# A planned Winograd kernel on Trainium2: the planner gives each PSUM bank one reader at a time, and four smaller edits

## The chip, the cores and the metric

The kernel runs on one core of a Trainium2 chip. The metric is the device time of one execution in microseconds. The engines are named as in the profile: PE is TensorE's matmul and PEld its weight load, DVE is VectorE, ACT is ScalarE, POOL is GpSimd, and SP is SyncE, which issues most transfers.

## The reference

`x` is 1024 x 512, `weight` is 64 x 512 x 512 (embedding e, feature f, model m), `lin_w` is 512 x 512, all in fp32:

```python
out_lin = x @ lin_w.T + lin_b
xv = jnp.einsum('bf,efm->bem', x, weight)
zp = jnp.einsum('bf,efm->bem', jnp.square(x), jnp.square(weight))
interaction = 0.5 * jnp.sum(jnp.square(xv) - zp, axis=1)
return out_lin + interaction
```

The second product needs no e of its own: the sum over e of x^2 times w^2 is x^2 times the sum of w^2 over e. So the large work is `xv`, whose squares are summed over e.

## The kernel before, in words

**Tiles and groups.** The 512 columns m are cut into 22 groups (`groups`, line 149): two narrow ones of 16 columns and twenty wide ones of 24. With the 64 embeddings, half a wide group is 12 x 64 = 768 columns of weights. The batch is cut into two halves of 512 rows (four blocks of 128), the features into two halves of 256 (two blocks of 128).

**Outer level.** Of each group, the 2 x 2 blocks of x times the 2 x 2 blocks of the weight are multiplied with seven products in place of eight (Winograd's form of Strassen's scheme), numbered 1 to 7 and run in the `ORDER` 1, 6, 5, 2, 7, 4, 3 (line 19). The sums of blocks of x (`X1` to `X7`) are made once. The sums of weights come by DMAs that add into SBUF (`outer_sum`, line 696, through `dma_add`, line 470), issued from GpSimd's queue; so do two sums of results (`outer_out`, line 707: ob += od after product 7's tree, oc += od after product 4's).

**Inner level.** Each outer product has a tree of its own. Products 6, 4 and 3 of every group, and all seven of a narrow one, go through `tree` (line 737): seven inner products of two matmuls each, 384 columns in a wide group. Products 1, 5, 2 and 7 of wide groups go through `wide_tree` (line 826): twenty inner products of one matmul of 256 columns. The sums of weight pieces (tile `t`) are made on GpSimd. fp32 matmuls stand in the profile as two records each.

**PSUM.** Four tiles `b1`, `b3`, `b2_0`, `b2_1` of two banks each take the products. The single banks are `b_l` and `b_r` in the profile (`alone=True`, line 379), the pair is `b`. A product is added in place onto what a bank holds; what must be kept is copied to another bank or to SBUF (`p5`, `p53`: `p` in the profile) by ScalarE (`copy`, line 443, shown as L446 or L447), and results leave by VectorE's adds (`tt`, line 429, shown as L437), which may also run on GpSimd when no operand is in PSUM. Matmuls are at line 480, or 537 for the two ends.

**`EARLY` and `HOLD`.** For outer products in `EARLY` (line 21), `tree` adds the addend of the result's last quarter to bank b3 right after inner product 5 (`leave(3, "b3")`, line 797) and adds bank b2 later (`more(3, b2)`, line 817). For the others, line 799 copies b3 to a p5 tile and line 819 adds bank and tile first, then the addend. Product 4's addend is `oc`, its target `oa` (lines 732 and 733).

**After the trees.** ScalarE squares the results and VectorE sums the squares over e into `acc` (`finish`, line 722, shown as L454 and L463). `w_squares` (line 713) does the same to the raw weights, into `w2_sum`.

**The two ends.** `lin` (line 614) computes the linear part first, and the end (from line 1005) computes x^2 times `w2_sum`, both by `outer_products` (line 595): seven products `big` (line 529) of sixteen records each per block product, on pairs of banks, with the copies u2 <- b1 and u3 <- u2 between them. At the end the linear part and half of `acc` are first added up (`add_acc`, line 1048, shown as L1051), the sums of squares of x are made by `tt` and `minus_both` (line 581, shown as L584, VectorE alone), and `leave` (line 1088) adds the products and stores the output.

**What sets the order.** No order is written by hand. `Plan` (line 153) holds every operation with a cost per engine, and `order` (line 191) plays the engines against each other and emits the operations in the order that comes out; on the chip each engine then runs its own in that order. PE's operations have keys (their place in the sequence) and may run ahead of it by at most `AHEAD` = 20 us when a lower key is not ready. For all others the planner works out the latest start that does not hold up PE, moved by the table `AHEAD_OF` (line 41, in eighths of a us by operation). `ready` (line 231) tells when an operation can start:

```python
        def ready(o):
            return max([0.0] + [d.end for d in o.waits]) + self.HOP
```

It knows of data and of buffers, not of two engines that read one bank at the same time. In the emitted program two such readers do run one after the other, as the trace shows. `APART` (line 252 and 258) keeps VectorE's operations of two SBUF operands that are marked `both` apart from GpSimd's; `add_acc` isn't marked.

Of the kernel before, what the change touches and what calls it, by code (L numbers as in the profile page):

```python
# [20 lines left out]
EARLY = (2, 4, 6, 7)  # L21
# [20 lines left out]
0:c 1:348h 2:2hcy 3:347k 4:3498 5:2hq1 6:2hlv 7:2h68 8:1muu 9:2h1k a:1mst b:2haa c:1wij d:2gyq e:1qxb f:l05  # L42
g:yb9 h:1aj i:5b4 j:29s4 k:-16 l:b m:l n:6 o:-v p:g q:2t r:d s:-9 t:-l u:1t v:ts w:1a x:c y:-n z:19 10:-k
11:4uw 12:-a 13:-10 14:-37 15:1o 16:n 17:-x 18:-14 19:m 1a:13 1b:-g 1c:18 1d:-6 1e:90j 1f:-e 1g:-1f 1h:3n 1i:i
1j:39 1k:-2z 1l:e 1m:-i 1n:-1g 1o:m 1p:35 1q:n 1r:-1 1s:-u 1t:-g 1u:13 1v:-3 1w:-2 1x:-3u 1y:-18 1z:-9 20:-2
21:s 22:m 23:-h 24:-y 25:u 26:-d 27:-31 28:3 29:u 2a:h 2b:17 2c:-s 2d:-o 2e:s 2f:b 2g:14 2h:1q 2i:26 2j:-i
2k:1i 2l:-4 2m:-2f 2n:z 2o:9 2p:-4 2q:15 2r:46 2s:44 2t:q 2u:-a 2v:-q 2w:-a 2x:1r 2y:-1m 2z:g 30:-19 31:-2o
32:8 33:14 34:-b 35:17 36:1t 37:-14 38:6 39:3 3a:-o 3b:-2 3c:-1o 3d:17 3e:-19 3f:1a3 3g:-7 3h:i 3i:-1j 3j:1md
3k:-15 3l:x 3m:128 3n:r 3o:-a 3p:-13 3q:-8 3r:h 3s:b 3t:-16 3u:-a 3v:1mh 3w:-9 3x:4 3y:-14 3z:-e 40:1t8 41:-f
42:e 43:1p 44:-k 45:1l 46:1g 47:-4 48:m 49:-13 4a:12 4b:-d 4c:-24 4d:-k 4e:r 4f:1 4g:-z 4h:i 4i:h 4j:1i 4k:c  # L50
4l:g 4m:9 4n:o 4o:-1f 4p:1e 4q:-3 4r:-1i 4s:f 4t:x 4u:-f 4v:-18 4w:-12 4x:1p8 4y:q 4z:-2e 50:-w 51:9 52:-1j
53:-10 54:5 55:3 56:1fd 57:r 58:a 59:1 5a:-12 5b:-2 5c:-6 5d:1r 5e:l 5f:-27 5g:8 5h:-15 5i:-5 5j:-n 5k:2g 5l:a
5m:-o 5n:p 5o:10 5p:1 5q:1b 5r:-l 5s:1bb 5t:-1 5u:-1o 5v:10 5w:-1 5x:2y 5y:-3 5z:5 60:1d 61:15 62:-d 63:5
64:-5 65:x 66:d 67:3 68:-w 69:-1r 6a:-z 6b:v 6c:ct 6d:-2t 6e:-j 6f:-2 6g:-6 6h:-t 6i:r 6j:-1f 6k:f 6l:d 6m:-1n
6n:b 6o:9 6p:5 6q:-5 6r:-22 6s:-3 6t:j 6u:-f 6v:h 6w:-6 6x:p 6y:-d 6z:-l 70:m 71:-c 72:-x 73:-y 74:-d 75:-v
76:m 77:-1 78:7 79:1a 7a:22 7b:a 7c:-2 7d:-v 7e:-2 7f:-k 7g:g 7h:-z 7i:-18 7j:-1b 7k:-13 7l:-17 7m:-o 7n:-u
7o:h 7p:z 7q:-5 7r:j 7s:-v 7t:6 7u:-u 7v:s 7w:i 7x:-v 7y:-1e 7z:-f 80:s 81:u 83:-j 84:-m 85:-7 86:-1e 87:f
88:2 89:1 8a:-1c 8b:-g 8c:-4 8d:-1y 8e:-j 8f:-u 8g:-5 8h:c 8i:-6 8j:-2 8k:-3 8l:-3 8m:-l 8n:s 8o:1c 8p:h
8q:-2e 8r:-e 8s:96 8t:-3 8u:6 8v:18 8w:17 8x:-3 8y:-1g 8z:-3 90:-5 91:-r 92:18 93:-1 94:3c 95:12 96:-s 97:-3
98:-15 99:p 9a:-e 9b:-15 9c:1b 9d:-1f 9e:9 9f:13 9g:g 9h:1k 9i:-17 9j:12 9k:b 9l:-28 9m:d 9n:c 9o:-6 9p:-5  # L60
9q:1 9r:-f 9s:x 9t:3 9u:-q 9v:12 9w:-13 9x:-q 9y:-r 9z:-u a0:-18 a1:-a a2:-8 a3:-1h a4:-17 a5:-w a6:1pg a7:-d
a8:-1 a9:-1c aa:-j ab:1a ac:e ad:-x ae:-6 af:-i ag:i ah:z ai:r aj:1r ak:8 al:-1h am:-35 an:-c ao:-5 ap:-z aq:x
ar:3 as:e at:1 au:g av:-c aw:w ax:-j ay:-u az:1r b0:6 b1:38 b2:1v b3:j b4:-10 b5:4 b6:15 b7:33 b8:-1 b9:-1
ba:-1d bb:1f bc:-2q bd:-c be:-16 bf:-c bg:1dx bh:18 bi:a bj:b bk:t bl:2 bm:8 bn:1x bo:-r bp:-o bq:f br:11
bs:-i bt:-2 bu:9 bv:-1x bw:-h bx:b by:-y bz:s c0:7 c1:1b c2:1v c3:i c4:-m c5:q c6:11 c7:7 c8:-x c9:-y ca:3
cb:d cc:-1p cd:1 ce:a cf:-1l cg:-17 ch:-q ci:-3 cj:56 ck:f cl:-1z cm:s cn:-1f co:w cp:-u cq:i cr:j cs:12 ct:5
cu:y cv:-l cw:-k cx:1 cy:-1e cz:-q d0:k d1:r d2:d d3:x d4:-q d5:-10 d6:o d7:-5 d8:1q d9:-r da:-a db:-2 dc:d
dd:-3 de:-3 df:-1p dg:-16 dh:l di:-l dj:-3q dk:18 dm:g dn:1y do:-z dp:-4 dq:-4 dr:-1c ds:c dt:-17 du:-fq dv:-a
dw:-bz dx:1m dy:-j dz:-1e e0:-20 e1:1s e2:1l e3:-1w e4:-1p e5:4 e6:j e7:-x e8:-19 e9:19 ea:1n eb:1g ec:-3
ee:13 ef:15 eg:-1o eh:-19 ei:2m ej:i ek:-x el:1d em:-a en:-4 eo:1i ep:-1z eq:-1t er:-1a es:15 eu:-c ev:a  # L70
ew:-1s ex:1f ey:2m ez:-t f0:1c f1:-y f2:-8 f3:g f4:-4 f5:-1m f6:83 f7:3 f8:-173 f9:t fa:-d fb:a fc:4 fd:20n
fe:b ff:-v fg:t fh:-n fi:34 fj:fq fk:-o fl:-l fm:-3 fn:-10 fo:-g fp:197 fq:e fr:-1g fs:1y ft:z fu:-w fv:-2v
fw:l fx:-1b fy:-1x fz:-19 g0:-l g1:-2 g2:36 g3:g g4:g g5:s g6:-5 g7:x g8:24 g9:m ga:h gb:q gc:-8 gd:o ge:-14
gf:f gg:-z gh:1 gi:k gj:-8 gk:v gl:19j gm:-d gn:z go:9 gp:a gq:i gr:-2 gs:-6 gt:6 gu:-1s gv:e gw:15 gx:-2
# [64 lines left out]
1ce:-c 1cf:x 1cg:12 1ch:4 1ci:-w 1cj:15 1ck:-2d 1cl:-f 1cm:-13 1cn:-21 1co:12 1cp:-32 1cq:-1j 1cr:2g 1cs:-1x  # L139
1ct:-6 1cu:-a 1cv:k 1cw:-l 1cx:n 1cy:i 1cz:-1t 1d1:14 1d2:-i 1d3:-q 1d4:-p 1d5:-k 1d6:-p 1d7:-4 1d8:-1 1d9:15  # L140
1da:-1z 1db:18 1dc:-9 1dd:s 1de:k 1df:-u 1dg:z 1dh:-f 1di:bj 1dj:-5 1dk:26 1dl:1 1dm:-6 1dn:8 1do:n 1dp:-d
1dq:-3 1dr:-28 1ds:x 1dt:n 1du:-c 1dv:j 1dw:v
"""
AHEAD = 20.0
APART = True
# [1009 lines left out]
```

## Time and profile before

| what | us |
|---|---|
| median of 3 runs | 1438.69 |
| lowest and highest run | 1434.45, 1439.11 |
| the profiled execution | 1437.59 |
| its span in the profile | 1435.8 |
| PE busy | 1409.5 |
| DVE busy | 1224.1 |
| POOL busy | 1088.4 |
| ACT busy | 792.7 |

The span is the time from the first to the last instruction of the profiled execution, whose own time is a little longer. The granted TensorE clock was 0.999 of full speed. In the rows that follow, a timeline row reads: start and length in us, engine, line, operation, what it writes and reads, shape, how often, and in brackets the engine's idle time before it with what ended it. A row of groups ends with busy us, mean ns of one, and the idle time before them. A row of waits gives the total, the number and the longest. A row of the chain gives start, length and what ran. A row of stretches gives the stretch, its length, then the busy time of PE, PEld, DVE, ACT and POOL with the number of records, the granted clock, the DMA share and GB/s.

### The profile page before, as it was taken

The numbers are of one execution on the slowest core, as the hardware profiler recorded it, in microseconds if no ns is written. First come the engines' busy times: TensorE is split into PE (matmuls) and PEld (weight loads), VectorE is DVE, ScalarE is ACT, GpSimd is POOL, SyncE is SP. The second block draws the span as 40 slices with busy tenths as digits, with TensorE's granted clock in tenths as the row PEclk, the third lists the DMA queues.
The fourth block names the chain that finished last, engine by engine and source line by source line (L and its number), as shares of the span: only waits on it lengthen the run. The fifth ranks groups of instructions, "written<-read, shape, count | busy, mean of one in ns | idle before, by whom it ended". The sixth has DMA issues, their size and how long they took to land.

```text
span 1435.8 us, 17687 instructions
## 1 busy us (share of the span) xinstructions
PE 1409.5 (98%) x5504; PEld 1024.8 (71%) x5504; DVE 1224.1 (85%) x1809; ACT 792.7 (55%) x1296; POOL 1088.4 (76%) x1067
## 2 busy tenths in 40 slices
PE   9999999999999999999999999999999999999988
PEld 7777767767676776767677676767677676767756
DVE  6577888888988888898889889888988988988887
ACT  3255465656646565665656465555646555565732
POOL 6999876877687777778787777778777687778760
PEclk9999999999999999999999999999999999999999
DMA  8779577684948678495957859595775959485672
GB/s 259 177 167 236 144 180 175 161 217 107 251 124 209 156 180 196 115 246 118 233 145 172 202 128 235 112 250 130 182 190 145 218 117 260 114 199 146 168 174 81
DMA packets 98542, 251.84 MB, mean 175 GB/s; under 512 B 29521, under 2 KB 39249, under 8 KB 98449
## 3 DMA queue, kind: packets, MB, share of 16 engines
q0 software_dynamic: 26448, 134.49, 48.0%
q1 hardware_dynamic: 70848, 115.17, 23.0%
q10 hardware_dynamic: 1152, 1.05, 0.2%
q8 instruction: 45, 0.74, 0.2%
q14 instruction: 49, 0.39, 0.1%
HBM read 127.04 MB, written 6.19 MB: 93 GB/s over the span
## 4 chain that ended last, share of the span: by engine, by line
PE 80%; POOL 6%; DMA 6%; DVE 3%; ACT 3%; issue 2%; SPq 0%; ACTq 0%; POOLq 0%; DVEq 0%
PE b L480 36%; PE b_r L480 22%; PE b_l L480 20%; POOL t L437 3%; PE b L537 2%; DVE oa L437 2%; POOL X L437 1%; DMA oc<-od 1%; DMA ob<-od 1%; DMA w<-T 1%; DMA ob<-lin_wT 1%; ACT b_l L447 1%; DVE w_sum L463 1%; DMA T<-weight 1%; ACT od L446 1%
## 5 line engine op out<-in xcount | busy, mean ns | idle before, releaser
L480 PE MATMUL b<-t,X 128*128 128x384 f32 (+1 forms) x1184 | 400.7, 471 | 5.9 <-DVE oa L437 3.4
L437 POOL TENSOR_TENSOR t<-t,w 128x512 f32<-128x512 f32 (+1 forms) x300 | 294.9, 991 | 113.2 <-PE b L480 86.8
L480 PEld LDWEIGHTS b<-t,X 128*128 128x128 f32 x1184 | 218.8, 190 | 133.6 <-POOL t L437 12.7
L480 PE MATMUL b_l<-t,X 128*128 128x256 f32 x960 | 247.6, 381 | 0.4 <-ACT b_l L447 0.3
L480 PE MATMUL b_r<-t,X 128*128 128x256 f32 x800 | 225.6, 386 | 3.7 <-ACT b_l L447 1.1
L480 PEld LDWEIGHTS b_l<-t,X 128*128 128x128 f32 x960 | 180.7, 190 | 37.9 <-ACT b_l L447 5.5
L437 POOL TENSOR_TENSOR t<-w 128x768 f32<-128x768 f32 (+1 forms) x88 | 162.9, 1851 | 50.5 <-DMA w<-T 28.9
L480 PEld LDWEIGHTS b_r<-t,X 128*128 128x128 f32 x800 | 145.6, 190 | 60.3 <-issue 16.2
L454 ACT ACTIVATE oa<-oa 128x768 f32<-128x768 f32 (+1 forms) x176 | 143.8, 824 | 78.5 <-DVE oa L437 77.8
L454 ACT ACTIVATE wsq<-w 128x768 f32<-128x768 f32 (+1 forms) x132 | 108.5, 823 | 127.0 <-DMA w<-weight 85.3
L463 DVE TENSOR_REDUCE w_sum<-wsq 128x12 f32<-128x768 f32 (+1 forms) x176 | 161.4, 920 | 1.5 <-ACT wsq L454 1.0
L463 DVE TENSOR_REDUCE acc<-oa 128x12 f32<-128x768 f32 (+1 forms) x176 | 158.5, 920 | 4.0 <-ACT oa L454 3.8
L480 PE MATMUL b_r<-w,X 128*128 128x256 f32 x600 | 152.2, 384 | 2.3 <-DVE oa L437 1.4
L480 PEld LDWEIGHTS b_r<-w,X 128*128 128x128 f32 x600 | 110.5, 190 | 31.6 <-issue 6.7
L480 PE MATMUL b_l<-w,X 128*128 128x256 f32 x480 | 121.1, 385 | 1.3 <-ACT b_l L447 1.2
L447 ACT COPY b<-b 128x768 f32<-128x768 f32 (+2 forms) x78 | 59.8, 767 | 95.3 <-PE b L480 53.2
L480 PE MATMUL b<-w,X 128*128 128x384 f32 (+1 forms) x336 | 107.6, 456 | 1.3 <-DMA w<-T 1.3
L480 PEld LDWEIGHTS b_l<-w,X 128*128 128x128 f32 x480 | 88.6, 190 | 21.9 <-ACT b_l L447 9.6
L437 DVE TENSOR_TENSOR ob<-b,oa 128x768 f32<-128x768 f32 (+1 forms) x88 | 80.4, 930 | 15.2 <-PE b L480 7.4
L437 DVE TENSOR_TENSOR oa<-b,oc 128x768 f32<-128x768 f32 (+1 forms) x88 | 80.9, 930 | 14.1 <-PE b L480 12.6
L480 PE MATMUL b<-T,X 128*128 128x384 f32 (+1 forms) x264 | 90.8, 478 | 1.6 <-ACT oa L447 1.3
L454 ACT ACTIVATE oc<-oc 128x768 f32<-128x768 f32 (+1 forms) x88 | 69.9, 819 | 37.1 <-DMA oc<-od 37.1
(150 smaller groups left out, 2530.6 us busy)
## 6 DMA issues: line engine op xcount, KB each, us to landing
w<-weight SPq DMA_DIRECT2D x120, 384.0 KB, 6.6
ob<-od POOLq DMA_DIRECT2D x40, 768.0 KB, 8.6
oc<-od POOLq DMA_DIRECT2D x40, 768.0 KB, 11.6
T<-weight SPq DMA_DIRECT2D x40, 384.0 KB, 5.1
w<-T POOLq DMA_DIRECT2D x20, 768.0 KB, 6.8
T1a<-weight SPq DMA_DIRECT2D x20, 384.0 KB, 3.3
T1a<-weight POOLq DMA_DIRECT2D x10, 768.0 KB, 9.0
w22a<-weight SPq DMA_DIRECT2D x20, 384.0 KB, 10.9
```

What stands on the lines that cost most here:

```text
L437: return f(o.ap, a.ap, b.ap)
L446: return nc.scalar.activation(o.ap, i.ap, AF.Copy, scale=-1.0)
L447: return nc.scalar.copy(o.ap, i.ap)
L454: lambda _: nc.scalar.activation(o.ap, i.ap, AF.Square), i.atoms, o.atoms)
L463: nc.vector.tensor_reduce(o, x, axis=AX.X, op=ALU.add)
L480: nc.tensor.matmul(a.ap, b.ap, w.ap, start=start, stop=True, skip_group_check=True)
L537: nc.tensor.matmul(a.ap, b.ap, w(k).ap, start=first and k == 0 and j % 2 == 0, stop=True, skip_group_check=True)
```

## The change

It has these parts:

- The planner: an operation that touches a PSUM bank is ready only when the last operation of another engine (PE's apart) that it has placed on that bank has ended. The hop between engines is 0.19 in place of 0.18 us; an accumulating DMA occupies its queue 2.8 in place of 2.5 us per 1024 columns and becomes ready 0.35 us later. The table `AHEAD_OF` is another, of 104 lines in place of 101.
- Product 4 is no longer in `EARLY`: its tree copies b3 to a p5 tile.
- Both ends: products 1, 2, 6 and 7 are issued by bank halves as product 3 was, and the two copies are made one bank at a time.
- The end: the sums of squares that were `minus_both` are `tt`, so that GpSimd may make them, and the signs of the weights' sums (`zsum`) and of the final adds change to fit.

The diff, without the table:

```diff
@@ -18,7 +18,7 @@
 SEG = 128
 ORDER = (1, 6, 5, 2, 7, 4, 3)
 HK = (1, 5, 2, 7)
-EARLY = (2, 4, 6, 7)
+EARLY = (2, 6, 7)
 
 SLOT = {1: 0, 7: 1, 2: 2, 4: 3, 5: 4, 6: 5, 3: 6}
 PLACE = {5: -6, 3: -2, 1: 0, 6: 3, 2: 4, 7: 6, 4: 9}
@@ -39,107 +39,110 @@
 P5S = 2
 P53S = 2
 AHEAD_OF = """
...
 """
 AHEAD = 20.0
 APART = True
@@ -151,7 +154,7 @@
 
 
 class Plan:
-    HOP = 0.18
+    HOP = 0.19
 
     def __init__(self):
         self.ops = []
@@ -164,10 +167,10 @@
         self.part, self.count = part, 0
 
     def add(self, costs, emit, reads=(), writes=(), key=None, land=0.0, both=False,
-            banks=(), queue=0.0):
+            banks=(), queue=0.0, lag=0.0):
         op = SimpleNamespace(
             n=len(self.ops), costs=costs, emit=emit, key=key, land=land,
-            deps=set(), succ=[], latest=None, end=None, both=both, banks=banks, queue=queue,
+            deps=set(), succ=[], latest=None, end=None, both=both, banks=banks, queue=queue, lag=lag,
         )
         for r in reads:
             if r in self.writer:
@@ -222,14 +225,15 @@
         free = dict.fromkeys(pending, 0.0)
         running = dict.fromkeys(pending)
         times = [self.HOP]
-        done, late, adding = [], 0.0, 0.0
+        done, late, adding, using = [], 0.0, 0.0, {}
 
         def release(o):
             for e in o.costs:
                 pending[e].add(o.n)
 
-        def ready(o):
-            return max([0.0] + [d.end for d in o.waits]) + self.HOP
+        def ready(o, e):
+            locked = [x.end for at, _, _ in o.banks for f, x in using.get(at, {}).items() if f != e]
+            return max([0.0] + [d.end for d in o.waits] + locked) + self.HOP + o.lag
 
         def longer(e, by):
 
@@ -245,11 +249,11 @@
         def pick(e, now):
             if e == PE:
                 able = [n for n in pending[e]
-                        if ops[n].due < now - late + AHEAD and ready(ops[n]) <= now + 1e-6]
+                        if ops[n].due < now - late + AHEAD and ready(ops[n], e) <= now + 1e-6]
                 return ops[min(able, key=lambda n: (ops[n].key, n))] if able else None
             if APART and e == POOL and free[DVE] > now + 0.1 and running[DVE].both:
                 return None
-            at = {n: ready(ops[n]) for n in pending[e]}
+            at = {n: ready(ops[n], e) for n in pending[e]}
             for n in sorted((n for n in at if at[n] <= now + 1e-6),
                             key=lambda n: (ops[n].latest, n)):
                 o = ops[n]
@@ -294,6 +298,9 @@
                     o.begin, free[e] = now, now + cost
                     running[e] = o
                     o.end = free[e] + o.land
+                    if e != PE:
+                        for at, _, _ in o.banks:
+                            using.setdefault(at, {})[e] = o
                     if o.queue:
                         adding = max(adding, free[e]) + o.queue
                         o.end = adding + o.land
@@ -471,7 +478,7 @@
         def emit(_):
             nc.gpsimd.dma_start(o, i, accum_op=ALU.add)
 
-        plan.add({POOL: 0.7}, emit, reads + writes, writes, land=1.8, queue=2.5 * rows / 1024)
+        plan.add({POOL: 0.7}, emit, reads + writes, writes, land=1.8, queue=2.8 * rows / 1024, lag=0.35)
 
     def mm(o, x, w, start, key):
         plan.add(
@@ -595,20 +602,26 @@
     def outer_products(xs, ws, base_key, ready, leave):
 
         u2, u3, m4, m5 = "b2_0", "b1", "b3", "b2_1"
-        big("b1", xs[1], ws[1], True, base_key)
-        copy(pair(u2), pair("b1"))
-        big("b1", xs[2], ws[2], False, base_key + 1)
+        halves = ((0, 0, 2), (1, 0, 2), (0, 2, 4), (1, 2, 4))
+
+        def copy_pair(o, i):
+            for k in range(2):
+                copy(reg(o, k * N, N), reg(i, k * N, N))
+
+        big("b1", xs[1], ws[1], True, base_key, halves)
+        copy_pair(u2, "b1")
+        big("b1", xs[2], ws[2], False, base_key + 1, halves)
         leave(0, 0, "b1")
         big(m4, xs[4], ws[4], True, base_key + 2)
         ready(0, m4)
         big(m5, xs[5], ws[5], True, base_key + 3)
         ready(1, m5)
-        big(u2, xs[6], ws[6], False, base_key + 4)
-        copy(pair(u3), pair(u2))
-        big(u3, xs[7], ws[7], False, base_key + 5)
+        big(u2, xs[6], ws[6], False, base_key + 4, halves)
+        copy_pair(u3, u2)
+        big(u3, xs[7], ws[7], False, base_key + 5, halves)
         leave(1, 0, u3)
         leave(1, 1, u3)
-        big(u2, xs[3], ws[3], False, base_key + 6, ((0, 0, 2), (1, 0, 2), (0, 2, 4), (1, 2, 4)))
+        big(u2, xs[3], ws[3], False, base_key + 6, halves)
         leave(0, 1, u2)
 
     def lin():
@@ -1023,10 +1036,10 @@
                  x.atoms, x.atoms)
     xs = {1: x2[0, 0], 2: x2[0, 1], 4: x2[1, 1], 5: next(rooms), 6: next(rooms), 7: x2[1, 0],
           3: next(rooms)}
-    tt(xs[5], xs[4], x2[1, 0], True)
-    minus_both(xs[6], xs[5], xs[1])
+    tt(xs[5], xs[4], x2[1, 0])
+    tt(xs[6], xs[5], xs[1], True)
     tt(xs[7], xs[1], x2[1, 0], True)
-    minus_both(xs[3], xs[2], xs[6])
+    tt(xs[3], xs[2], xs[6], True)
 
     def quadrant(t, h, c, lo=0, hi=C):
         return t[:, 4 * h:4 * h + 4, c * C + lo:c * C + hi]
@@ -1063,10 +1076,10 @@
         return reg("w2_sum", q * KH * M + c * C, C, (M, KH))
 
     zsum = {i: next(spare) for i in (1, 2, 7, 4)}
-    tt(two(zsum[1]), w2(0, 1), w2(0, 0))
-    tt(two(zsum[2]), w2(1, 1), two(zsum[1]))
-    tt(two(zsum[4]), w2(1, 0), two(zsum[2]))
-    tt(two(zsum[7]), w2(0, 1), w2(1, 1))
+    tt(two(zsum[1]), w2(0, 1), w2(0, 0), True)
+    tt(two(zsum[2]), w2(1, 1), two(zsum[1]), True)
+    tt(two(zsum[4]), two(zsum[2]), w2(1, 0), True)
+    tt(two(zsum[7]), w2(1, 1), w2(0, 1), True)
 
     def w2_raw(q, c):
         return lambda k: reg("w2_sum", (q * KH + k) * M + c * C, C)
@@ -1080,17 +1093,17 @@
 
     def ready(c, b):
         if c == 0:
-            tt(rest[1, 0], rest[1, 0], pair(b), True)
+            tt(rest[1, 0], rest[1, 0], pair(b))
         else:
-            tt(rest[1, 1], rest[1, 1], pair(b))
-            tt(rest[0, 1], rest[0, 1], pair(b))
+            tt(rest[1, 1], rest[1, 1], pair(b), True)
+            tt(rest[0, 1], rest[0, 1], pair(b), True)
 
     def leave(h, c, b):
         r = rest[h, c]
         n = 1 if (h, c) != (0, 1) else 2
         for k in range(n):
             o = Reg(r.tile, r.off + k * 2 * N // n, 2 * N // n)
-            tt(o, o, reg(b, k * 2 * N // n, 2 * N // n), c == 0)
+            tt(o, o, reg(b, k * 2 * N // n, 2 * N // n), True)
             dma(out_dst[:, 4 * h + k * 4 // n:4 * h + (k + 1) * 4 // n, ts(c, C)],
                 o.ap.rearrange("p (a m) -> p a m", m=C), o.atoms, ())
 
```

More of the change, by code (lines that the diff above doesn't have):

```diff
@@ L41 @@
 AHEAD_OF = """
[L42 to L71, printed above, removed]
```

175 lines of the change are left out of this document (104 added, 71 removed).

## The prediction

> **What bounds the kernel now.** The page comes first: the span and the busy time of the engines.
>
> ```profile
> span 1435.8 us, 17687 instructions
> PE 1409.5 (98%) x5504; PEld 1024.8 (71%) x5504; DVE 1224.1 (85%) x1809; ACT 792.7 (55%) x1296; POOL 1088.4 (76%) x1067
> ```
>
> TensorE is the bound, but 98% says little about what is left, since the ends of matmul records are modelled. The distance from one matmul's start to the next is the better measure. The second view is the chain that ended last in order of time, and beside it the busy time of one stretch, for the number of records in it.
>
> ```profile
> 139.81 5.16 PE b L480 x16
> ...
> 1091.25 5.16 PE b L480 x16
> ...
> 1100.06 2.16 PE b_r L480 x10
> ...
> 1345.26 5.51 PE b L480 x16
> ```
>
> ```profile
> 1217.80:1281.00 63.20, 62.95 (x245) 45.03 (x244) 57.22 (x86) 38.02 (x62) 48.42 (x47) 1.00 0.70 171
> ```
>
> The same place of the pattern stands at 139.81 and at 1345.26, 19 wide groups later, so a group takes (1345.26 - 139.81) / 19 = 63.44 us. A record of 384 columns takes 5.16 / 16 = 0.3225 us, one of 256 columns 2.16 / 10 = 0.216 us. By the code a wide group has 80 products of 256 columns and 42 matmuls of 384, two records each: 160 x 0.216 + 84 x 0.3225 = 61.65 us, and the stretch does hold about 244 records. So TensorE loses 1.79 us in each group, 36 us over the twenty, although the stretch calls it busy for 62.95 of 63.20. That is what the steady part can still give. VectorE stands at 57 of 63 us there, ScalarE at 38, GpSimd at 48.
>
> The third view is the timeline inside a group, at two of the places where TensorE starts late.
>
> ```profile
> 1109.08 0.68 DVE L437 TENSOR_TENSOR oa<-oa,b_l 128x512 f32<-128x512 f32 x1
> ...
> 1109.79 0.57 ACT L447 COPY b_r<-b_l 128x512 f32<-128x512 f32 x1 [0.23 <-DVE oa L437]
> ...
> 1110.39 0.69 DVE L437 TENSOR_TENSOR oa<-oa,b_l 128x512 f32<-128x512 f32 x1 [0.64 <-ACT b_r L447]
> ...
> 1110.69 1.03 PE L480 MATMUL b_r<-t,X 128*128 128x256 f32 x4
> ...
> 1111.00 0.74 DVE L437 TENSOR_TENSOR oa<-oa,b_r 128x256 f32<-128x256 f32 x2
> ...
> 1111.89 0.67 PE L480 MATMUL b_r<-w,X 128*128 128x256 f32 x2 [0.17 <-DVE oa L437]
> ```
>
> ```profile
> 1168.84 1.46 PE L480 MATMUL b_l<-t,X 128*128 128x256 f32 x6
> ...
> 1169.04 0.37 ACT L447 COPY p<-b_r 128x256 f32<-128x256 f32 x1
> ...
> 1169.44 0.42 DVE L437 TENSOR_TENSOR od<-b_r,p 128x256 f32<-128x256 f32 x1 [0.39 <-ACT p L447]
> ...
> 1169.90 0.38 ACT L446 ACTIVATE od<-b_r 128x256 f32<-128x256 f32 x1 [0.49 <-DVE od L437]
> ...
> 1170.43 0.67 PE L480 MATMUL b_r<-t,X 128*128 128x256 f32 x2
> ```
>
> In the first, VectorE reads the left bank, ScalarE's copy of the same bank waits for it, and VectorE's second read waits for the copy: two readers of one bank run one after the other. The planner before lets them run together, so it takes the bank for free earlier than it is. TensorE's four records from 1110.69 end their issue at 1110.69 + 4 x 0.216 = 1111.55; the next starts at 1111.89, 0.34 late, behind the VectorE reads of the bank's other half. In the second, the six from 1168.84 end at 1170.14 and the next starts at 1170.43, 0.29 late, behind ACT, DVE, ACT on one bank.
>
> The fourth view is the timeline of the end.
>
> ```profile
> 1385.82 4.93 DVE L1051 SCALAR_TENSOR_TENSOR X<-w,X 128x1024 f32<-128x1024 f32 x1
> 1386.71 2.96 POOL L437 TENSOR_TENSOR X<-w22a,X 128x1024 f32<-128x1024 f32 x1
> 1390.68 1.81 DVE L437 TENSOR_TENSOR oa<-b,oc 128x768 f32<-128x768 f32 x2
> ...
> 1391.68 2.92 PE L480 MATMUL b<-t,X 128*128 128x384 f32 x4 [3.39 <-DVE oa L437]
> ...
> 1394.40 1.59 PE L480 MATMUL b<-w22b,X 128*128 128x384 f32 x4
> ...
> 1396.64 1.22 DVE L1051 SCALAR_TENSOR_TENSOR X<-X,X 128x1024 f32<-128x1024 f32 x1
> ```
>
> An add of two SBUF operands that takes 1.22 us by itself took 4.93 us and ended 1.08 us after GpSimd's sum beside it. It stood ahead of the read that frees a bank of product 4's tree, and TensorE idled 3.39 us. The next four records then took 1394.40 - 1391.68 = 2.72 us in place of 4 x 0.3225 = 1.29, so 1.43 us more went with a slow restart. This one collision cost 4.82 us.
>
> **The change, part by part.** *One reader per bank in the planner* (with the hop of 0.19, the later start and slower queue of accumulating DMAs, and a new table of due times). No instruction is added; the order on all engines changes. Its field is the 1.79 us per group. The rows show one lost start of about 0.3 us behind readers of one bank in each of two groups; if the new order takes that one away, it gives 0.3 x 20 = 6 us. The far end on the good side is half of the loss, 18 us; on the bad side a second such start, +6 us. I take -6.5 (0.33 x 20, the larger row rounded), since the wait that the model lacked is in plain sight, and the other small losses in a group follow real chains (a product, a correction in the bank, a copy) that no model removes. What is late next is VectorE itself, at 90% of a group.
>
> *Product 4's first addend.* Before, the tree of product 4 adds oc to bank b3 at once and adds b2 later, two VectorE ops that read a bank. After, ScalarE copies b3 to a p5 tile, VectorE adds bank and tile, and the add of oc has SBUF operands alone, so it goes to GpSimd or VectorE. The tree of product 3 does that already and has the prices.
>
> ```profile
> L447 ACT COPY p<-b 128x768 f32<-128x768 f32 x20 | 16.0, 799 | 9.8 <-PE b L480 9.7
> L437 DVE TENSOR_TENSOR oa<-b,oc 128x768 f32<-128x768 f32 x80 | 75.5, 954 | 11.6 <-PE b L480 10.2
> L437 POOL TENSOR_TENSOR ob<-p,ob 128x768 f32<-128x768 f32 x20 | 36.5, 1823 | 10.0 <-DMA ob<-od 4.6 <-DVE p L437 4.0 <-DVE ob L437 1.4
> POOL t L437 <- PE b L480: 87.0, 30, 6.1
> ```
>
> Per group ScalarE gets 0.80 us, VectorE loses 0.95 and GpSimd gains 1.82 (or VectorE keeps its 0.95). The copy holds b3 no longer than the add did (0.80 against 0.95). The DMA that adds od into oc has to wait for oc's readers, but its second half waits for the tree's last add in either form, so it starts no later unless GpSimd is late with its add. On GpSimd the t sums and the issues of accumulating DMAs queue behind the 1.82 us; its stretch has 63.20 - 48.42 = 14.8 us idle, and it waited 87 us in all for TensorE to free room for t, which means that its sums run ahead. So I cost this part at nothing. Without that cover it would be up to 1.82 x 20 = 36 us; the other way, less work on VectorE could be worth one more lost start, 6 us.
>
> *Squares' sums on GpSimd.* In the end two sums of squares that only VectorE could do (about 1.2 us each) may now go to GpSimd, as two others could; the signs change with them, at no cost. They lie many products ahead of their use. What they can do is collide, as above. The new order has no cause to put a sum at that same place, and I let the 4.82 us go; if a collision returns, nothing.
>
> *Ends by bank halves.* Before, a copy of a whole pair stands between two products.
>
> ```profile
> 10.88 1.00 ACT L447 COPY b<-b 128x1024 f32<-128x1024 f32 x1
> ...
> 11.94 3.72 PE L537 MATMUL b<-ob,oa 128*128 128x256 f32 x16 [1.29 <-ACT b L447]
> ...
> 1423.55 3.69 PE L537 MATMUL b<-w,X 128*128 128x256 f32 x16 [1.18 <-issue]
> 1427.08 2.75 PE L537 MATMUL b<-w_sum,T1b 128*128 128x256 f32 x12
> ...
> 1429.87 0.69 DVE L437 TENSOR_TENSOR X<-X,b 128x512 f32<-128x512 f32 x1 [0.17 <-PE b L537]
> 1430.61 1.13 PE L537 MATMUL b<-w_sum,T1b 128*128 128x256 f32 x4 [0.78 <-DVE X L437]
> ```
>
> ```profile
> L447 ACT COPY b_r<-b_l 128x512 f32<-128x512 f32 x80 | 46.3, 578 | 18.9 <-PE b_l L480 14.0 <-DVE oc L437 3.0 <-DVE oa L437 1.8
> ```
>
> TensorE idles 1.29 us at the first such copy and 1.18 at the last, 2.47 in all. With copies by halves (0.58 us each) under the matmuls of the other bank, that could go whole. But product 3 is done by halves already, and its rows speak against it: VectorE's read of the left half started only when the twelfth record, in the right half, was through, and TensorE's last four, right half again, waited 0.78 us for that read to end. The pair behaves as one. So each half copy would hold TensorE for about 0.78 - (0.69 - 0.58) = 0.67 us, two of them 1.34 us against 1.29 or 1.18 now. I take 0; bounds -2.5 (the halves are free of each other) and 4 x 1.34 - 2.47 = +2.9 (all four copies of the two ends stall). The Trainium skill's page "PSUM — Partial Sum Buffer" (section "The four PSUM rules") has each bank as a memory of its own; by that rule the sum would be 2.5 us lower, and the trace does not agree here: the 0.78 us were waited between two different banks.
>
> The stretch from 80 to 140 us, where the groups turn from narrow to wide, idles more than the others.
>
> ```profile
> 80.00:140.00 60.00, 56.54 (x249) 45.74 (x248) 46.17 (x74) 32.71 (x61) 56.20 (x75) 1.00 0.82 196
> ```
>
> Its 3.5 us may shrink or double under a new order; I take 0.
>
> *Sum.* -6.5 - 4.8 + 0 + 0 + 0 = -11.3 us on the profiled execution's 1437.6: 1426.3. The runs' median, 1438.7, lies 1.1 above that execution, so the forecast for it is 1427.4 us.
>
> **The rivals.** (a) *The stalls only move.* The lost starts are small and many; a new order loses others, and the end has its own new wait. For it: three of four readers in the rows above are on TensorE's path only by tenths. Against: the mis-modelled wait is real. Then between 0 and 4.8 us are gained: about 1436.
> (b) *The readers were most of it.* Half of the 1.79 us goes, 18 us, and the 4.8: 1416. For it: two of the three reader waits shown also delay copies that later products need. Against: a correction in a bank is a chain of its own.
> (c) *GpSimd's sums hold VectorE up in the end: slower.* Four sums may now run there beside four adds of two SBUF operands on VectorE. Each that meets one ahead of a read that frees a bank costs 4.82 us; it decides from the second on, since one is there now. With two, and no gain in the groups: 1438.7 + 4.8 = 1443.5; with three 1448. For it: the 4.93 us row. Against: GpSimd has little else in the last 40 us and the adds are not all urgent. The Trainium skill's page "SBUF — State Buffer" (section "Who interferes with whom") has the pair of ports of GpSimd and VectorE as a lock that one holds for a whole instruction, which speaks against moving such sums to GpSimd; the trace agrees in that the add outlasted the sum.
> (d) *GpSimd's 1.82 us per group is not covered: slower.* It stands ahead of a t sum that TensorE is due for, with 0.6 us of it open in each group: +12, about 1445 with the end's gain. It decides when GpSimd's lead over TensorE falls under 1.8 us; the 87 us of waiting for room speak against it.
>
> **How the numbers follow.** Forecast 0.50 (its own range 1421 to 1433), (a) 0.21, (b) 0.13, (c) 0.09, (d) 0.07. A measurement here can tell about 0.3%, 4.3 us, from no change; the runs shown lie 4.7 apart. The forecast and (b) are faster by more than that, 0.63; (a) is the same, 0.21; (c) and (d) slower, 0.16. The range 1416 to 1441 leaves out (c), (d) and a little below (b).
>
> **What would show it.** Right: the same place of the pattern recurs every 63.1 us in place of 63.44; no wait of TensorE over 3 us in the end, and all adds of line 1051's kind near 1.2 us; one more copy to p of 0.80 us per group and, on GpSimd, one more add of 1.8; waits of TensorE near 0.7 us at each half copy of the ends. Wrong: a period of 63.44 or more, new waits of matmuls on GpSimd's t sums, the ends' halves without waits, or a long add of line 1051 ahead of a stalled matmul again.

## The result and the profile after

The changed kernel takes 1415.93 us (median of 4 runs, 1415.55 to 1416.58) against 1438.9 us for the kernel before (4 runs, 1434.45 to 1441.6): a ratio of 0.9844, with a 95% interval of 0.9819 to 0.9869. It is 23 us faster, twice the 11.3 us forecast. The profiled execution took 1416.58 us, its span is 1414.8 us.

The page of the kernel after, span and busy time of the engines:

```profile
span 1414.8 us, 17745 instructions
...
PE 1392.1 (98%) x5504; PEld 1035.1 (73%) x5504; DVE 1205.7 (85%) x1785; ACT 813.3 (57%) x1322; POOL 1132.2 (80%) x1091
```

PE is busy for the same 98%: that share says nothing of what was gained. The work moved as the diff says: DVE lost 18.4 us, POOL gained 43.8, ACT 20.6. The chain of the kernel after, at the places that were shown of the kernel before:

```profile
139.13 5.16 PE b L487 x16
...
1321.48 5.51 PE b L487 x16
```

Cut at these places, the whole difference can be laid out:

| stretch | before, us | after, us | difference |
|---|---|---|---|
| start, up to the place near 139 | 139.81 | 139.13 | -0.68 |
| 19 wide groups | 1205.45 | 1182.35 | -23.10 |
| from there to the end | 90.54 | 93.32 | +2.78 |
| span | 1435.8 | 1414.8 | -21.0 |

All of the gain lies in the groups: 1182.35 / 19 = 62.23 us each in place of 63.44. Over the 61.65 us that the records need to issue, a group now loses 0.58 us in place of 1.79. The start and the end together cost 2.1 us more. The rest of the 23 us lies outside the profiled pair: that of before ran 1.3 us under its median, that of after 0.7 over its own.

A stretch of one such period in the kernel after:

```profile
1197.25:1259.48 62.23, 62.23 (x246) 45.56 (x245) 54.71 (x84) 37.41 (x62) 50.49 (x48) 1.00 0.75 179
```

PE is busy for the whole of it, DVE for 54.71 us in place of 57.22, POOL for 50.49 in place of 48.42.

The timeline of the kernel after at the same place inside a group as the first one shown of the kernel before:

```profile
1090.01 0.57 ACT L454 COPY b_r<-b_l 128x512 f32<-128x512 f32 x1 [0.22 <-PE b_l L487]
1090.61 1.29 DVE L444 TENSOR_TENSOR oa<-oa,b_l 128x512 f32<-128x512 f32 x2 [1.10 <-ACT b_r L454]
...
1090.72 1.53 PE L487 MATMUL b_r<-t,X 128*128 128x256 f32 x6
...
1092.09 1.89 PE L487 MATMUL b_l<-w,X 128*128 128x256 f32 x8
```

Before, DVE read the bank, ACT's copy came second, DVE's next read third: two changes of reader. Now the copy is first and DVE's two reads follow in one run, so there is one. The six PE records end their issue at 1090.72 + 6 x 0.216 = 1092.02 and the next starts at 1092.09: 0.07 us late, where it was 0.34.

The end is where the forecast expected a collision to go. The timeline of the kernel after there:

```profile
1361.84 6.48 DVE L1064 SCALAR_TENSOR_TENSOR X<-X,X 128x1024 f32<-128x1024 f32 x1
...
1361.96 2.97 POOL L444 TENSOR_TENSOR X<-X,w22a 128x1024 f32<-128x1024 f32 x1
...
1364.26 2.96 POOL L444 TENSOR_TENSOR X<-w22a,X 128x1024 f32<-128x1024 f32 x1
...
1368.24 0.94 DVE L444 TENSOR_TENSOR oa<-b,oc 128x768 f32<-128x768 f32 x1
...
1369.24 6.90 PE L487 MATMUL b<-t,X 128*128 128x384 f32 x12 [4.50 <-DVE oa L444]
...
1375.97 2.74 PE L487 MATMUL b<-w22b,X 128*128 128x384 f32 x8
```

The add of `add_acc` meets two sums of GpSimd's in a row and takes 6.48 us in place of 4.93. It again stands ahead of the read that frees a bank; PE idles 4.50 us, and the next twelve records then take 1375.97 - 1369.24 = 6.73 us in place of 12 x 0.3225 = 3.87, 2.86 more. So this place costs 4.50 + 2.86 = 7.36 us, where it cost 4.82.

The bank halves, seen by PE in the timelines of the start and of the end, kernel after:

```profile
27.86 1.99 PE L544 MATMUL b<-w22b,X 128*128 128x256 f32 x8 [0.70 <-ACT b L454]
...
1397.22 2.75 PE L544 MATMUL b<-T1a,X 128*128 128x256 f32 x12
1400.68 1.13 PE L544 MATMUL b<-T1a,X 128*128 128x256 f32 x4 [0.70 <-ACT b L454]
```

Of the eight half copies, seven hold PE up, six for about 0.7 us and the first for 1.24; from start to start PE loses 1400.68 - 1397.22 - 12 x 0.216 = 0.87 us. The waits of PE for them in the kernel after (total, number, longest):

```profile
PE b L544 <- ACT b L454: 5.5, 7, 1.2
```

These seven make 5.5 us. Before, the waits for whole copies were 1.29 + 0.22 us at the start and 1.18 at the end, 2.7 in all, so the halves cost 2.8 us more. The waits of PE's b_r for DVE's oa, 1.4 us in 8 before, are not in the view any more.

### The profile page after: what moved, and what is told of

Its sections match the earlier page's. It is cut to its first block, busy times and chain, and to the rows that moved or that the text cites. A ratio compares the mean times of both kernels' runs of the same rounds, so it can differ in the third digit from the quotient of the medians.

```text
span 1414.8 us, 17745 instructions
## 1 busy us (share of the span) xinstructions
PE 1392.1 (98%) x5504; PEld 1035.1 (73%) x5504; DVE 1205.7 (85%) x1785; ACT 813.3 (57%) x1322; POOL 1132.2 (80%) x1091
## 4 chain that ended last, share of the span: by engine, by line
PE 91%; POOL 3%; DMA 2%; DVE 1%; ACT 1%; issue 1%; ACTq 0%; POOLq 0%; DVEq 0%
PE b L487 40%; PE b_r L487 24%; PE b_l L487 23%; PE b L544 3%; POOL t L444 2%; DMA oc<-od 1%; DMA w<-T 1%; DMA ob<-lin_wT 1%; DVE X L1064 0%; ACT b L454 0%; POOL oc L479 0%; DVE acc L470 0%; POOL oa L444 0%; POOL ob L479 0%; POOL ob L444 0%
## 5 line engine op out<-in xcount | busy, mean ns | idle before, releaser
L487 PE MATMUL b_r<-t,X 128*128 128x256 f32 x800 | 218.1, 383 | 0.2 <-ACT b_r L454 0.2
L444 POOL TENSOR_TENSOR t<-w 128x768 f32<-128x768 f32 (+1 forms) x88 | 159.1, 1809 | 68.2 <-DMA w<-T 28.7
L487 PE MATMUL b_r<-w,X 128*128 128x256 f32 x600 | 147.7, 379 | 0.3 <-ACT p L454 0.3
L487 PEld LDWEIGHTS b_r<-w,X 128*128 128x128 f32 x600 | 113.8, 190 | 16.2 <-ACT p L454 0.7
L454 ACT COPY b<-b 128x768 f32<-128x768 f32 (+1 forms) x82 | 60.0, 731 | 106.3 <-PE b L487 83.3
L487 PE MATMUL b_l<-w,X 128*128 128x256 f32 x480 | 116.3, 382 | 0.1
L454 ACT COPY b_l<-b_r 128x512 f32<-128x512 f32 x80 | 46.1, 577 | 99.8 <-PE b_r L487 58.2
L461 ACT ACTIVATE ob<-ob 128x768 f32<-128x768 f32 (+1 forms) x88 | 71.2, 820 | 30.2 <-DVE ob L444 26.7
```

Source lines behind the costliest of these rows:

```text
L444: return f(o.ap, a.ap, b.ap)
L454: return nc.scalar.copy(o.ap, i.ap)
L461: lambda _: nc.scalar.activation(o.ap, i.ap, AF.Square), i.atoms, o.atoms)
L487: nc.tensor.matmul(a.ap, b.ap, w.ap, start=start, stop=True, skip_group_check=True)
```

## The experiments

The theories, as the expectations name them. A: the planner's reader rule itself makes the groups shorter. B: the rule alone gives nothing, or makes it worse; what counts is the rest of the change in the groups, or all of it together. C: the two halves of a bank pair hold each other up because the program takes the pair as one thing, and this costs the ends about what it costs in waits. D: the long add in the end is the collision with GpSimd and costs about 7 us. E: it comes from the sums of squares that GpSimd now makes. F: product 4's edit is covered by other work and worth nothing by itself. "Rekeyed" means that `AHEAD_OF` has one entry per operation, and where an experiment adds or removes operations the entries were moved to the same operations, new ones getting none.

### The rule alone, in the kernel before

```diff
+        def ready(o, e):
+            locked = [x.end for at, _, _ in o.banks for f, x in using.get(at, {}).items() if f != e]
+            return max([0.0] + [d.end for d in o.waits] + locked) + self.HOP
```

(with the bookkeeping of `using`; table, hop, DMA figures and all operations are those of before)

> The kernel before with one part of the change alone: the planner's rule that a PSUM bank has one reader at a time. Its table of due times, the hop, the accumulating DMAs' figures and all operations are those of before. Theory A (the rule itself shortens the groups): the period falls from 63.44 us to 62.6 or less, and the time to about 1422. Theory B (the new table of due times, made for the new rule, does it): the period stays within 0.2 us of 63.44, about 1435 to 1440, or grows, since the old table was made for the old rule.

Measured: 1453.04 us (1451.01 to 1454.52), 1.0093 of before [1.0078, 1.0107]. The chain of this kernel:

```profile
140.50 5.16 PE b L484 x16
...
1358.36 5.45 PE b L484 x16
```

A group takes (1358.36 - 140.50) / 19 = 64.10 us, 0.66 more than before. The largest row of its waits of PE:

```profile
PE b_l L484 <- ACT b_l L451: 8.8, 10, 1.8
```

Those waits for ScalarE's copies of b_l were 1.4 us before. The waits of b_r for DVE's oa, 1.4 us in 8 before, fall to one of 0.5 us, but those of b_r for DVE's oc grow from 0.5 us in one to 3.5 in 9, and those for t sums (5.0 us) and weights (3.4 us) grow too. Theory A falls in its plain form: a truer model with a table that was fitted to the other model is slower.

### The kernel after without the rule

```diff
-            locked = [x.end for at, _, _ in o.banks for f, x in using.get(at, {}).items() if f != e]
+            locked = []
```

> The kernel after without that one rule; its table and all else are those of after. Theory A: the period goes back from 62.23 to about 63.4 us, about 1438. Theory B: the table carries most of the gain, the period stays under 62.6, about 1416 to 1422.

Measured: 1438.55 us (1436.76 to 1439.95), 0.9992 of before [0.9981, 1.0003]. The whole gain is gone. The chain of this kernel:

```profile
331.14 5.16 PE b L487 x16
...
1210.46 5.16 PE b L487 x16
...
1346.35 5.51 PE b L487 x16
```

From 331.14 to 1210.46 a group takes 62.81 us, from there to 1346.35 a group takes 67.95: the small losses are half back, and two long ones come. One of them in its timeline:

```profile
1265.10 1.82 DVE L444 TENSOR_TENSOR ob<-b,ob 128x768 f32<-128x768 f32 x2 [1.21 <-DMA ob<-od]
...
1266.11 2.93 PE L487 MATMUL b<-t,X 128*128 128x384 f32 x4 [4.41 <-DVE ob L444]
```

The read that frees PE's bank itself waited 1.21 us for an accumulating DMA, and PE 4.41 us for the read, with a slow restart (four records in 2.72 us). What the rule itself does shows at one place inside a group. First the kernel after, then this kernel, which has the same operations and the same table:

```profile
1086.93 0.37 ACT L454 COPY p<-b_r 128x256 f32<-128x256 f32 x1 [0.44 <-PE b_r L487]
1087.20 0.39 ACT L453 ACTIVATE od<-b_r 128x256 f32<-128x256 f32 x1
...
1087.59 1.46 PE L487 MATMUL b_r<-t,X 128*128 128x256 f32 x6
1087.62 0.42 DVE L444 TENSOR_TENSOR od<-b_r,p 128x256 f32<-128x256 f32 x1 [0.67 <-ACT od L453]
...
1088.89 1.89 PE L487 MATMUL b_l<-t,X 128*128 128x256 f32 x8
```

```profile
1098.83 0.37 ACT L454 COPY p<-b_r 128x256 f32<-128x256 f32 x1 [0.44 <-PE b_r L487]
1099.24 0.42 DVE L444 TENSOR_TENSOR od<-b_r,p 128x256 f32<-128x256 f32 x1 [0.39 <-ACT p L454]
...
1099.50 1.77 PE L487 MATMUL b_r<-t,X 128*128 128x256 f32 x6
...
1099.70 0.38 ACT L453 ACTIVATE od<-b_r 128x256 f32<-128x256 f32 x1 [0.49 <-DVE od L444]
...
1100.45 0.60 ACT L454 COPY b_l<-b_r 128x512 f32<-128x512 f32 x1
...
1101.10 1.89 PE L487 MATMUL b_l<-t,X 128*128 128x256 f32 x8
```

With the rule ScalarE reads the bank twice and VectorE follows. Without it the two take turns, ScalarE, VectorE, ScalarE, as in the kernel before; ScalarE waits 0.49 us for VectorE, its copy into b_l ends at 1101.05, and PE's next records start 1101.10 - 1099.50 - 6 x 0.216 = 0.30 us late. With the rule they start on time: 1087.59 + 6 x 0.216 = 1088.89.

Theory A's time came, about 1438, though not its even period. Neither the rule with the old table (+13 us) nor the new table and the edits without the rule (0) have the gain; the pair has it. Both runs join a planner to a table that was made for another one, so how much is the rule's and how much the lost fit, they don't say.

### All four without a table

To see the parts without a table that is fitted to something else, four kernels have it empty.

```diff
-AHEAD_OF = """
...
-"""
+AHEAD_OF = ""
```

The kernel before so:

> The kernel before with an empty table: every operation is due exactly when the planner's backward pass says. It is the base for the next three. All theories: slower than 1439; with a table that doesn't fit its operations, e8 had groups of 66.1 us and 1499, so about 1480 to 1520.

With the rule beside it, as in the first experiment:

> The same, empty table, with the rule of one reader per bank alone. Theory A (the rule is worth something by itself, on an order that no table shapes): 15 us or more less than the run with the empty table and without the rule. Theory B (only the table made for the rule brings the gain; the rule alone just moves the order): within 10 us of it, either way.

With product 4's edit instead, `EARLY = (2, 6, 7)`:

> The kernel before with an empty table and product 4 taken out of EARLY, nothing else. Theory F (that edit is covered): within 5 us of the run with the empty table alone. Rival (it frees VectorE and b3): 10 us or more less, that is 0.5 us or more per group.

And the whole kernel after:

> The kernel after with an empty table. Theory A: most of the 23 us between before and after is there without any table too: 15 us or more under the kernel before with an empty table. Theory B: under 10 us of difference, the table of after carries the gain, and it is worth more than the table of before was.

| without a table | us | lowest to highest | against the first |
|---|---|---|---|
| before | 1564.18 | 1559.82 to 1567.93 | |
| before with the rule | 1577.08 | 1571.39 to 1580.22 | +12.9 |
| before with product 4's edit | 1537.15 | 1533.5 to 1539.78 | -27.0 |
| after | 1510.63 | 1508.67 to 1514.84 | -53.6 |

The tables are worth 1564.18 - 1440.66 = 124 us before (1440.66 is the kernel before, run beside these) and 1510.63 - 1415.93 = 95 us after, several times the change itself. The first was expected at 1480 to 1520 us, too low. The rule alone is slower here too, by a little more than theory B allows and against theory A. Product 4's edit is worth 27 us, against theory F. The whole change is worth more than the 15 us of theory A here, though not through the rule alone. The waits of PE without product 4's edit and with it, some of the largest rows of each:

```profile
PE b L378 <- POOL t L335: 18.3, 12, 2.1
...
PE b_r L378 <- DVE ob L335: 12.6, 18, 1.5
PE b_r L378 <- ACT oa L344: 12.2, 9, 2.4
```

```profile
PE b_l L378 <- ACT b_l L345: 17.2, 21, 1.3
...
PE b L378 <- POOL t L335: 3.9, 11, 0.7
```

The waits for t sums fall from 18.3 to 3.9 us, those of b_r for DVE's ob and ACT's oa vanish, others grow. -27.0 and +12.9 don't add up to -53.6: the parts work on each other, or the hop and the DMA figures count, which were not tried by themselves. Each of these is also one order out of many, so a single difference is no pure price of one edit.

### Product 4 back in `EARLY`, in the best kernel then known

The base is the kernel after with `add_acc` kept apart (the next experiment), the table rekeyed.

```diff
-EARLY = (2, 6, 7)
+EARLY = (2, 4, 6, 7)
```

> The kernel of e4 with product 4 back in EARLY, the due times of the same operations kept: per group one copy of 0.80 us less on ScalarE, the add of 1.82 us off GpSimd, 0.95 us more on VectorE. Theory F (this edit is covered, worth nothing by itself): the period stays at 62.2 us and the time within 3 us of e4's 1409.0. Rival (it frees VectorE or bank b3 and part of the shorter group is its): the period goes up by 0.2 to 0.6 us, 1413 to 1421.

Measured: 1499.29 us (1498.91 to 1499.6), 1.0414 of before [1.0397, 1.0431]. In its chain the same place of the pattern stands at 209.61 and, 18 groups later, at 1399.10: (1399.10 - 209.61) / 18 = 66.08 us per group, 3.9 more than its base: worse than the kernel before, which has this very form of product 4. That is the table without its operations, not the price of the edit, so this run is inconclusive on what product 4 is worth in the tuned kernel.

### `add_acc` kept apart from GpSimd's sums

```diff
-                reads + r.atoms, r.atoms,
+                reads + r.atoms, r.atoms, both=True,
```

> The kernel after, its planner told that the adds of half of acc (two operands in SBUF) must not run beside GpSimd's work, as it knows of others; nothing else. Theory D (in after such an add, 6.48 us long beside two sums on GpSimd, holds up the read that frees a bank): all these adds near 1.2 us, no wait of TensorE over 2 us in the end, about 7 us less, 1409. Rival (the end is late for another reason, a DMA or the chain of results): the wait moves to another operation and the time stays within 2 us of 1416.

Measured: 1408.95 us (1408.29 to 1409.28), 0.9786 of before [0.9773, 0.9799]; 7.0 us less than the kernel after, with the groups at the same 62.23. Its timeline at the place of the collision:

```profile
1363.40 1.45 PE L487 MATMUL b<-w22b,X 128*128 128x384 f32 x4
1363.67 0.95 DVE L444 TENSOR_TENSOR oa<-b,oc 128x768 f32<-128x768 f32 x1
1364.53 1.61 DVE L1064 SCALAR_TENSOR_TENSOR X<-X,X 128x1024 f32<-128x1024 f32 x1
...
1364.69 2.83 PE L487 MATMUL b<-t,X 128*128 128x384 f32 x8
```

The add takes 1.61 us and comes behind the read, and PE goes on at 1364.69 = 1363.40 + 4 x 0.3225. Theory D holds in mechanism and size (7.36 us by the rows). Its signs are not all met: the add is still above 1.22 us, with one of GpSimd's sums beside it until 1365.05, and a wait of 2.18 us for weights stays ahead of this place, as in the kernel after (2.19).

### The sums of squares on VectorE alone

```diff
-    tt(xs[5], xs[4], x2[1, 0])
-    tt(xs[6], xs[5], xs[1], True)
+    tt(xs[5], xs[4], x2[1, 0], only=DVE)
+    tt(xs[6], xs[5], xs[1], True, DVE)
```

(and the same for `xs[7]` and `xs[3]`; base: the kernel after)

> The kernel after with the four sums of squares in the end held to VectorE; nothing else. Theory E (the sums on GpSimd are what the long add waits for): the long add falls to near 1.3 us, the wait of 4.5 us in the end goes, about 7 us less than after's 1415.9, 1409; VectorE's four sums of 1.2 us each cost little of that. Rival (GpSimd's other work, its sums of weights and its DMA issues, holds the add as well): an add of 3 us or more stays ahead of a stalled matmul, 1413 to 1416.

Measured: 1411.73 us (1410.38 to 1412.34), 0.9804 of before [0.9788, 0.9821]; 4.2 less than the kernel after. In its timeline the add has its price:

```profile
1362.67 1.22 DVE L1064 SCALAR_TENSOR_TENSOR X<-X,X 128x1024 f32<-128x1024 f32 x1
```

Theory E holds for the mechanism. Two things account for most of what is short of 7 us: a wait for a half copy at 1395.76 is 1.57 us long in place of 0.71, and the records behind a wait for weights, from 1355.44 to 1360.24, take 1.8 us more than their 3.01, where the same records of the kernel after, from 1356.14, take 0.26 more.

### Both ends whole, then the last end alone whole or free

First all of the ends as before, on the kernel after (table rekeyed):

```diff
-        big("b1", xs[1], ws[1], True, base_key, halves)
-        copy_pair(u2, "b1")
+        big("b1", xs[1], ws[1], True, base_key)
+        copy(pair(u2), pair("b1"))
```

(and the same for products 2, 6 and 7)

> The kernel after with both ends as before: products 1, 2, 6 and 7 by pairs of banks, the two copies of each end whole. All else, the due times of the same operations too, is that of after. Theory C (a pair of banks is waited for as one, so each half copy holds TensorE for 0.87 us, seven times in after): those seven waits, 6.7 us with one of 1.4, give way to three of 0.4 to 1.5 as in before, 3.2 us; 3 us less, about 1413. Rival (the halves hide the copies and the waits have another cause): 2 us more, about 1418.

Measured: 1427.73 us (1426.73 to 1428.47), 0.9917 of before [0.9904, 0.9931], 11.8 more than after. In its chain the same place stands at 338.21 and, 16 groups later, at 1332.39: 62.14 us per group, much as in the kernel after. But the kernel after reaches that place at 327.29: 10.9 us are lost where the table, made for the other start, no longer fits (one wait of 3.13 us for weights at 179.64, several near 1). So the total tells nothing of the halves. The waits do: the view has three for whole copies, 2.9 us, in place of seven for half copies, 5.5.

So the next two leave the start alone and change only the last end, on the kernel with `add_acc` apart. One has it whole; the other issues the same halves, but names each bank by a tile of its own:

```diff
-            outs = [reg(o, j * C, C) for j in range(j0, j1)]
+            outs = [bank(o, j // 2, j % 2 * C, C) for j in range(j0, j1)]
...
-                copy(reg(o, k * N, N), reg(i, k * N, N))
+                copy(bank(o, k), bank(i, k))
...
-            tt(o, o, reg(b, k * 2 * N // n, 2 * N // n), True)
+            for j in (k,) if n == 2 else (0, 1):
+                z = Reg(r.tile, r.off + j * N, N)
+                tt(z, z, bank(b, j), True)
```

> The kernel of e4 with the last end alone as before: pairs of banks, its two copies whole; the first end stays by halves, so that the groups' order is not touched. Theory C (a pair of banks is waited for as one): the three waits of 0.87 us in the end (at 1380, 1393 and 1396 us of e4) go, one of about 1.3 comes back: 1 to 1.5 us less than e4's 1409.0, about 1407.7. Rival (the halves do help): 1 to 2 us more, about 1410.5.

Measured: 1411.49 us (1410.42 to 1414.08), 0.9807 [0.9789, 0.9825]. Its timeline:

```profile
1363.40 4.27 DVE L1061 SCALAR_TENSOR_TENSOR X<-X,X 128x1024 f32<-128x1024 f32 x1
...
1368.59 5.83 PE L465 MATMUL b<-t,X 128*128 128x384 f32 x12 [2.29 <-DVE oa L422]
...
1399.32 3.69 PE L522 MATMUL b<-w,X 128*128 128x256 f32 x16 [1.18 <-issue]
```

The whole copy costs one wait of 1.18 us, but the order changed and the long add is back (4.27 us although it is marked: the mark keeps it from GpSimd's sums in the plan, on the chip they met). Inconclusive for the total.

> The kernel of e4, its last end by halves, but every matmul, copy and read of that end names a single bank's tile in place of half of a pair's (VectorE's reads of a pair become two of a bank each, six more operations and 0.17 us each). Theory C: with nothing that ties the two banks together the three waits of 0.87 us and the last one of 0.94 us go: 2.5 to 3.5 us less than e4, about 1406. Rival (the waits come from the copies' own lateness): the waits stay, 1409 or, with VectorE's extra operations, 1410.

Measured: 1405.02 us (1404.81 to 1407.17), 0.9763 of before [0.9746, 0.9780]; 3.9 less than its base, a little more than theory C's 2.5 to 3.5. PE in its last timeline:

```profile
1387.91 1.89 PE L541 MATMUL b_l<-T1a,X 128*128 128x256 f32 x8
1389.63 1.89 PE L541 MATMUL b_r<-T1a,X 128*128 128x256 f32 x8
...
1394.81 1.89 PE L541 MATMUL b_l<-w_sum,T1b 128*128 128x256 f32 x8
1396.54 1.89 PE L541 MATMUL b_r<-w_sum,T1b 128*128 128x256 f32 x8
```

No wait is left in this end, and each row starts 8 x 0.216 us behind the last. The tiles lie in the same banks as the pair did, so it was not the memory that held PE: theory C is shown for this end. By the Trainium skill's page "PSUM — Partial Sum Buffer" (section "The four PSUM rules") each bank is a memory of its own; once the program names the banks apart, the trace agrees.

This is the fastest kernel of the study: 34 us under before, 11 under after.

## Why the prediction was right or wrong

**The sign and the range.** Faster was forecast and came. The time, 1415.93 us, lies at the range's low end, 0.07 us below it, and on rival (b)'s 1416. That it meets this number is luck: the rival's sum was 18 from the groups and 4.8 from the end, the measured one is 23.1 from the groups and a loss of 2.8 in the end.

**The step that failed: "I take -6.5 (0.33 x 20, the larger row rounded)".** The groups, which hold this term and product 4's, moved by -23.1. The step counted one late start per group and set the rest aside: "the other small losses in a group follow real chains (a product, a correction in the bank, a copy) that no model removes".

But PE's rows, start to start, show more of the same size in those very groups of the kernel before: 0.20, 0.34 and 0.29 us at 1107.01, 1111.89 and 1121.88 in the one, 0.12, 0.29, 0.16 and 0.27 us at 1161.94, 1170.43, 1173.68 and 1184.17 in the other. In the four groups from 964.55 on, the starts of 0.12 us or more make 0.83 to 0.98 us per group and all late starts above 0.045 us make 1.56 to 1.75. In four groups of the kernel after, from 948.79, 1073.02, 1135.1 and 1197.25, none is later than 0.11 us, and all together make 0.44 to 0.52. So every one of the larger ones went, about 17 us in twenty groups, and a third of the small ones. Not all were readers: the start at 1111.89 is behind a change of reader, as the prediction says, and those at 1107.01 and 1170.43 behind ScalarE and VectorE taking turns on a bank, but those at 1121.88 and 1184.17 are behind VectorE's own queue, where a sum over e of 0.95 us (from 1119.87) or 0.94 us (from 1182.51) stands ahead of the operations on the bank. Two thirds of the 1.79 us went, more than the "far end" of half; the loss per group was the better bound.

What made the better order is only partly settled. Without the rule the gain is lost (1438.55), and readers take turns again; with the rule but without the other parts there is a loss (1453.04). So with this table the rule is needed, and with the old table it does not suffice. (A table made anew for the planner without the rule, or for the kernel before with it, was not tried.) Rival (b)'s name for it, the readers, is therefore half right.

**"So I cost this part at nothing".** Product 4's addend was worth 27 us where no table shaped the order; the bound that the prediction wrote for the good side was 6. How much of the 23 us is its own in the tuned kernel stays open, since the run that put it back broke the table. The reasons given for no cost held: the copies to p are 40 of 799 ns, and GpSimd's add has its price and its cover. The groups of the kernel after:

```profile
L454 ACT COPY p<-b 128x768 f32<-128x768 f32 x40 | 32.0, 799 | 34.1 <-PE b L487 34.1
...
L444 POOL TENSOR_TENSOR oa<-oa,oc 128x768 f32<-128x768 f32 x20 | 37.5, 1877 | 6.6 <-ACT oa L461 3.6 <-issue 3.0
```

The add is 1.88 us (1.82 forecast), and all 20 run on GpSimd: `tt` gives a sum of two SBUF operands to GpSimd alone unless `only=DVE` is said, so VectorE could not have kept it. And the view of PE's waits has none for a t sum any more, so rival (d) did not come. What the step left out is a gain: without a table the edit gave 27 us, more than the 20 x 0.95 = 19 us of VectorE's time that it takes away. By which waits the order gained, the runs don't show.

**"The new order has no cause to put a sum at that same place, and I let the 4.82 us go".** Wrong. The collision came back at nearly the same place, 1414.8 - 1361.84 = 53.0 us ahead of the end in place of 50.0, with two sums in place of one, and cost 7.36; the experiment that marks the add gave 7.0 back. There was a cause: `add_acc` was not marked, the planner prices it as if alone, and the change put two more sums on GpSimd, where `tt` sends them without a choice. One of the two beside the long add, at 1361.96, is such a sum; before, VectorE made it, at 1395.51. It is rival (c)'s mechanism, in the one place that was there already; (c) needed a second that TensorE waits for. A second long add did come, 2.71 us at 1375.69 beside another of GpSimd's sums, but PE did not wait for it.

**The halves.** The mechanism was right: 0.70 to 0.72 us of idle at six half copies, against 0.67 worked out. The size taken, 0, was not: seven of the eight half copies stalled PE, and the two ends cost 2.8 us more, against an upper bound of 2.9.

**The start** came at -0.68 us, although its halves cost 3.37 - 1.51 = 1.9 us more; the stretch from 80 to 140 us and what lies ahead of it gave back about 2.5. Its own cause was not looked into.

## What to carry to other kernels

A table of due times is fitted to one set of operations and one model of the machine: change a rule, an operation or a figure of the model and judge it only with a table made anew, or without any, since here the runs whose table didn't fit took 12 to 90 us more than their bases, while the changes themselves are worth 4 to 27. Price a scheduling change by the loss per period between first starts (1.79 us here), and list every late start of a period before you set any aside. Splitting a copy into bank halves paid here once each bank was a tile of its own to the program, and a VectorE operation of two SBUF operands ahead of a read that frees a bank has to be kept away from GpSimd's sums.

## What the runs showed of the hardware that was not expected

One VectorE add of two SBUF operands lasted through two GpSimd sums in a row: it started at 1361.84, 0.12 us ahead of the first, and ended at 1368.32, 1.10 us behind the second; 6.48 us for what takes 1.22 alone. It did not get its turn between them.

TensorE's clock can fall after idle times shorter than the long ones above. Two stretches of the kernel with the last end whole, after PE's wait of 2.29 us (the granted clock is the third number from the right):

```profile
1368.60:1371.00 2.40, 2.40 (x6) 1.50 (x7) 2.40 (x3) 0.71 (x1) 2.16 (x2) 0.79 0.99 200
1371.00:1374.20 3.20, 3.20 (x7) 1.72 (x6) 1.54 (x3) 0.14 (x1) 3.12 (x4) 0.62 0.98 196
```

The clock is 1.00 ahead of the wait, from 1362 to 1366, and 0.79 and then 0.62 behind it; twelve records took 1374.26 - 1368.59 = 5.67 us in place of 3.87. The Trainium skill's page "TensorE: Matmul & The Clock Gate" (Part 1, "The HAM clock gate") puts the fall to half rate behind about 3.4 us of idle; here the clock fell behind a wait of 2.29 us. But the length of the wait alone doesn't decide it. In the kernel with the sums of squares on VectorE, the clock was 0.77 and then 0.52 behind a wait of 2.06 us for weights, at 1355.44. In the kernel with `add_acc` apart, the same records start behind a wait of 2.18 us:

```profile
1356.25 1.56 PE L487 MATMUL b<-w,X 128*128 128x384 f32 x4 [2.18 <-DMA w<-T]
```

There the clock stayed at 1.00, and the next row starts at 1357.65, 1.40 us on for records that need 1.29. So a wait of a little over two microseconds cost 1.8 us more for the restart in two kernels and almost nothing in a third; what decides between them is not shown.
